# Table scatters in four pairs, each released by a cast on ScalarE, in a routed-expert transformer layer

## The chip, the cores and the metric

The kernel runs on one core of a Trainium2 chip. The metric is the device time of one execution in microseconds (us), as the median of several runs. The engines of the core are TensorE (PE, matmuls), VectorE (DVE), ScalarE (ACT), GpSimd (POOL) and SyncE (SP, which here issues most of the plain DMA transfers). Each works through its own queue in order and waits for the others by semaphores.

## The reference, cut to what matters

Eight sequences of 512 tokens with 256 features pass a cross attention (16 heads) and then a mixture of eight experts, of which each token takes its two best. Everything is float32.

```python
x = x + tanh(g_xattn[0]) * xattn(layernorm(x), ctx, ctx, mask, wq, bq, wk, bk, wv, bv, wo, bo)
x_flat = layernorm(x).reshape(-1, D)                 # 4096 tokens, D = 256
probs = softmax(x_flat @ router_w + router_b)        # E = 8 experts
top_w, top_idx = top_k(probs, 2)
comb = sum(top_w[..., None] * one_hot(top_idx, E), axis=1)
for e in range(E):
    h = gelu(x_flat @ expert_up[e].T)                # 1024 wide
    output = output + comb[:, e:e+1] * (h @ expert_down[e].T)
x = x + tanh(g_ffn[0]) * output
```

## The kernel before

**Routing by a table in HBM.** The kernel computes for each token only its two experts. When the router's choice for a batch (one sequence, four tiles of 128 tokens) is known, each of the batch's 1024 token-expert pairs gets a place in a table in HBM: the expert's region plus the number of pairs that the expert has so far. `place` (L343 to L374) works these places out. PE counts along the partitions (L348, L349), ACT copies the counts (L351), and POOL adds the running totals `filled` (L354, L355), picks the two places per token (L359 to L366, result `at`), writes the entries (token numbers L368, weight L371), and casts all eight columns of places to integers (L374, `place_i`). `enter(t)` (L376 to L382) then scatters tile t's entries, two indirect DMAs on POOL's queue (L378), one for each of the token's two choices. A batch has four such calls, so eight scatters.

**Expert jobs.** Experts are computed in jobs s of at most 256 table lines. Job s passes these steps:
- `list_rows(s)`, list(s) for short: SP reads the job's lines from the table (L690) into `listed`. It waits for every scatter that stands ahead of it in the program, and a scatter that stands behind it waits until it has read.
- `load(s)`: SP loads the expert's matrices up(s) and down(s), 1 MB each (L702, L703); there are three buffers.
- `fetch(s)`: POOL gathers the normalized token rows xg(s) by two indirect DMAs (L708); `turn(s)`: PE transposes them (L724), DVE copies them out (L726).
- `ups(s)`: PE multiplies with up (L736, h_ps, five PSUM banks), ACT applies GELU (L740, hT).
- `fetch_y(s)`: POOL gathers the rows of the output so far, y(s), by two indirect DMAs (L708). They must find the rows that job s-1 wrote.
- `downs(s)`: for each half of the job PE multiplies with down (L754, o_ps, two PSUM banks shared with other work), DVE scales and adds to y (L757), and POOL scatters the rows back (L760): out(s), two halves.

**The order of the work.** `attend_near` (L808) runs rounds b = -1 to 7. Round b does attention of batch b, prepares batch b+1 and b+2, projects and routes batch b-1, and enters batch b-2 into the table. A round has four groups g and in each three places n; a plan says which steps stand at (g, n) (L952 to L1003). The expert steps of jobs 0 to 3 stand at fixed groups of rounds 4 to 7 (`amid`, L1015 to L1030): the first lists at the end of round 4 (`begin`, L1006), list(5) and list(6) at the start of round 7's last group. Jobs from 4 on run after the last round, in what is called the tail here (L1080 to L1092); there the rest of batch 7's routing, and the placing and entering of batches 6 and 7, are taken from a queue, one step after each expert step. Entering before the change:

```python
for place, enter, counts in behind_route:
    plan[0, 2].append(place)
    if counts:
        plan[0, 2] += enter + counts
    else:
        for where, step in zip(((0, 2), (1, 0), (1, 1), (1, 2)), enter):
            plan[where].append(step)
```

`counts` are the planner's steps (L614 to L671), on DVE, that decide which lines a stage of jobs takes; they come with batches 2, 5 and 7. The order in which an engine's instructions are issued is made by a scheduler from this program: it may move an instruction ahead or back where data allows it, unless the instruction is wrapped in `keep_in_program_order`, which holds it at its place among its engine's instructions. The four `enter` calls were not held so, and on POOL all eight scatters of batches 0 to 5 ended up side by side behind the cast L374.

Only this branch runs with the inputs at hand (the mask's window is narrow); `attend_anywhere` (L1095) uses the same `finish` but isn't executed.

Of the kernel before, what the change touches and what calls it, by code (L numbers as in the profile page):

```python
# [24 lines left out]
QT = S // P  # L25
# [38 lines left out]
def flamingo_layer(ctx: ExitStack, tc: tile.TileContext, a: dict, out: bass.AP):  # L64
    nc = tc.nc
# [80 lines left out]
    place_i = fixed([P, B * QT, 2], "place_i", I32)  # L146
# [94 lines left out]
    def shared(p2, small, bank):  # L241
# [39 lines left out]
        def finish(b):  # L281

            x2T = p2.tile([P, DC, S], F32, tag="xnT", name=f"x2T{b}", bufs=1)
            said = {}

            def t3(name, dtype=F32):
                return small.tile([P, QT, E], dtype, tag=name, name=f"{name}{b}", bufs=2)

            def t2(name):
                return small.tile([P, QT], F32, tag=name, name=f"{name}{b}", bufs=2)  # L290

            def keep_rows(xn):
                nc.sync.dma_start(out=token_rows(rows, b), in_=xn)

            def keep_x():
                nc.sync.dma_start(out=token_rows(out, b), in_=xs[b])

            def logits():

                ps = bank(f"route_ps{b}")[:, :P]  # L300
                for dc in range(DC):
                    for t in range(QT):
                        nc.tensor.matmul(
                            ps[32 * t : 32 * t + 32, :], lhsT=rw[:, dc, :], rhs=x2T[:, dc, t * P : (t + 1) * P],
                            start=(dc == 0), stop=(dc == DC - 1),
                        )
                said["lgT"] = small.tile([P, P], F32, tag="lgT", name=f"lgT{b}", bufs=1)
                nc.scalar.copy(said["lgT"], ps)

            def route():  # L310
                ps = bank(f"lg_ps{b}")[:, :P]
                nc.tensor.transpose(ps, said["lgT"], ident)
                lg = t3("lg")
                nc.vector.tensor_tensor(
                    lg, ps.rearrange("p (t e) -> p t e", t=QT)[:, :, :E], over_t(rb), ALU.add
                )
                mx = t2("mx")
                nc.vector.tensor_reduce(mx, lg, AX.X, ALU.max)
                nc.vector.tensor_tensor(lg, lg, over_e(mx), ALU.subtract)
                pr = t3("pr")  # L320
                nc.scalar.activation(pr, lg, AF.Exp)
                sm = t2("sm")
                nc.vector.tensor_reduce(sm, pr, AX.X, ALU.add)
                rs = t2("rs")
                nc.vector.reciprocal(rs, sm)
                nc.vector.tensor_tensor(pr, pr, over_e(rs), ALU.mult)
                top = t3("top")
                idx = t3("idx", U32)
                for t in range(QT):
                    nc.vector.max(top[:, t, :], pr[:, t, :])  # L330
                    nc.vector.max_index(idx[:, t, :], top[:, t, :], pr[:, t, :])
                ix = t3("ix")
                nc.vector.tensor_copy(ix, idx)
                picks = small.tile([P, QT, 2, E], F32, tag="picks", name=f"picks{b}", bufs=2)
                nc.vector.tensor_tensor(
                    picks, iota.unsqueeze(1).unsqueeze(1).to_broadcast([P, QT, 2, E]),
                    ix[:, :, :2].unsqueeze(3).to_broadcast([P, QT, 2, E]), ALU.is_equal,
                )
                both = t3("both")
                nc.vector.tensor_tensor(both, picks[:, :, 0, :], picks[:, :, 1, :], ALU.add)  # L340
                said["top"], said["picks"], said["both"] = top, picks, both

            def place():  # L343

                both = said["both"].rearrange("p t e -> p (t e)")
                ps = bank(f"place_ps{b}")
                n = QT * E
                nc.tensor.matmul(ps[:, :n], lhsT=before, rhs=both, start=True, stop=True)  # L348
                nc.tensor.matmul(ps[:, n : 2 * n], lhsT=ones, rhs=both, start=True, stop=True)  # L349
                counts = small.tile([P, 2, QT, E], F32, tag="counts", name=f"counts{b}", bufs=2)  # L350
                nc.scalar.copy(counts.rearrange("p i t e -> p (i t e)"), ps[:, : 2 * n])  # L351
                place = t3("place")
                for t in range(QT):
                    nc.gpsimd.tensor_tensor(place[:, t, :], counts[:, 0, t, :], filled, ALU.add)  # L354
                    nc.gpsimd.tensor_tensor(filled, counts[:, 1, t, :], filled, ALU.add)  # L355
                mine = slice(b * QT, (b + 1) * QT)
                at = small.tile([P, QT, 2], F32, tag="at", name=f"at{b}", bufs=2)
                picked = said["picks"]
                nc.gpsimd.tensor_tensor(  # L359
                    picked, picked, place.unsqueeze(2).to_broadcast([P, QT, 2, E]), ALU.mult  # L360
                )
                for k in (4, 2, 1):
                    nc.gpsimd.tensor_tensor(
                        at.unsqueeze(3) if k == 1 else picked[..., :k], picked[..., :k], picked[..., k : 2 * k],
                        ALU.add,
                    )  # L366
                entry = entries[:, b % 2]
                nc.gpsimd.tensor_copy(  # L368
                    entry[:, :, :, :2], tokens_i[:, mine].unsqueeze(2).unsqueeze(3).to_broadcast([P, QT, 2, 2])
                )  # L370
                nc.gpsimd.tensor_scalar(  # L371
                    entry.bitcast(F32)[:, :, :, 2], said["top"][:, :, :2], tg[:, 1:2], None, ALU.mult
                )
                nc.gpsimd.tensor_copy(place_i[:, mine, :], at)  # L374

            def enter(t):  # L376
                for i in range(2):
                    nc.gpsimd.indirect_dma_start(  # L378
                        out=table_parts[2 * t + i][:, :],
                        out_offset=bass.IndirectOffsetOnAxis(ap=place_i[:, t, i : i + 1], axis=0),  # L380
                        in_=entries[:, b % 2, t % QT, i, :], in_offset=None,
                    )  # L382

            places = [place] + [lambda t=t: enter(t) for t in range(b * QT, (b + 1) * QT)]
            return x2T, keep_x, keep_rows, logits, route, places

# [421 lines left out]
    def attend_near(att):  # L808
# [230 lines left out]
        for b in range(-1, B):  # L1039
            if b + 3 < B:  # L1040
                load_x(b + 3, p2)
            if b + 3 < B:
                load_win(b + 3)
            if b == -1:
                clear_table(p2.tile([P, S], I32, tag="raw", name="none", bufs=1))
            behind_route = list(later)
            later.clear()
            if b == 0:
                looks, settle = normalize((2, "a", lambda: xnT[2]))
            plan = between(*(n if 0 <= n < B and (b, n) != (-1, 2) else None for n in (b - 1, b + 2, b + 3)))  # L1050
            if b == 0:
                plan[0, 0] += looks
                plan[0, 1].insert(0, settle)
            for place, enter, counts in behind_route:
                plan[0, 2].append(place)
                if counts:
                    plan[0, 2] += enter + counts
                else:
                    for where, step in zip(((0, 2), (1, 0), (1, 1), (1, 2)), enter):
                        plan[where].append(step)  # L1060
            for g in range(4):
                c, i = g // 2, g % 2
                if b >= 0:
                    pT = weights_T(b, c, i)
                work = deque(amid.get((b, g), []))
                for n in range(3):
                    if n == 0 and behind is not None:
                        weigh(*behind)
                    if n == 1 and b + 1 < B:
                        find_tops(b + 1, c, i)  # L1070
                    if n == 2 and g >= 2 and b + 1 < B:
                        lower_tops(b + 1, 0, g - 2)
                    if n == 2 and g < 2 and b >= 0:
                        lower_tops(b, 1, g)
                    for _ in range(-(-len(work) // (3 - n))):
                        work.popleft()()
                    for step in plan[g, n]:
                        step()
                behind = (b, c, i, pT) if b >= 0 else None
# [340 lines left out]
```

## Time and profile before

| what | us |
|---|---|
| median of 3 runs (lowest, highest) | 834.48 (833.77, 834.83) |
| the profiled execution | 850.71 |
| its span, first to last instruction | 848.9 |
| PE busy | 767.4 |
| DVE busy | 326.6 |
| POOL busy | 313.8 |
| ACT busy | 253.6 |
| 64 table scatters L378 on POOL | 62.7 (0.98 each) |
| 8 casts L374 on POOL | 0.19 each |
| first and last table scatter | 134.3, 447.9 |

Times within the execution are counted from the start of the span. A line of a timeline gives start, duration, engine, line of the kernel, operation, what it writes and reads, the shape, how many were merged, and in brackets the idle time ahead of it on its engine and what ended it ("issue": nothing that the profile shows). A line of the table by stretches gives from:to, the length, the busy time of PE, PE's weight loads, DVE, ACT and POOL with counts, the granted PE clock (1.00 is full), the share of the DMA engines, and GB/s. The busy shares, the granted clock and the DMA traffic over the span in 40 slices of 21.2 us:

```profile
PE   3786989888889999999997899999999999999992
DVE  7486887877865747524230111101011101011100
ACT  2434555453635435253311112121211111111210
POOL 2021115151645252545464453534353433434332
PEclk9788998998989999999999899999999999999997
DMA  4700001120292314063647557575666775747511
```

Each digit is a tenth. Up to slice 12 (250 us) PE and DVE are both busy, then DVE and ACT thin out as expert jobs take over, and from slice 22 on PE works through the jobs with everything else beside it. The scatters lie in slices 6 to 21.

### The profile page before, as it was taken

Reading aid. Unit: us, or ns where it says so; the run is one execution under the profiler, and the core shown is the slowest. Engines: PE = TensorE matmul, PEld = TensorE weight load, DVE = VectorE, ACT = ScalarE, POOL = GpSimd, SP = SyncE. Lnnn points to the kernel's source line nnn. Section 1 sums busy time; section 2 is a strip of 40 time slices with the busy share of each in tenths; the row PEclk is TensorE's granted clock in tenths of the full one; section 3 lists DMA queues with packets and bytes.
Section 4 is the critical chain, followed back from the end, with each engine's and each line's share of the span. In section 5 each row is a group of like instructions: output and inputs, shape, how many; then the busy total and the mean of one; then the engine's idle time right before and its main releaser. Section 6 shows DMA issues by size and latency. Waiting matters only on the chain. (4 is left out here: it accounts for less than half of the span.)

```text
span 848.9 us, 11331 instructions
## 1 busy us (share of the span) xinstructions
PE 767.4 (90%) x4090; PEld 568.3 (67%) x4090; DVE 326.6 (38%) x958; ACT 253.6 (30%) x485; POOL 313.8 (37%) x422
## 2 busy tenths in 40 slices
PE   3786989888889999999997899999999999999992
PEld 1343544444446575668786788888898988788882
DVE  7486887877865747524230111101011101011100
ACT  2434555453635435253311112121211111111210
POOL 2021115151645252545464453534353433434332
PEclk9788998998989999999999899999999999999997
DMA  4700001120292314063647557575666775747511
GB/s 143 259 7 1 32 32 32 47 68 12 87 316 95 106 53 125 4 211 94 215 133 261 197 162 244 171 240 164 228 183 227 219 253 169 243 164 245 198 50 36
DMA packets 87910, 121.58 MB, mean 143 GB/s; under 512 B 16798, under 2 KB 71713, under 8 KB 87841
## 3 DMA queue, kind: packets, MB, share of 16 engines
q1 hardware_dynamic: 75184, 93.44, 33.1%
q0 software_dynamic: 11840, 26.76, 10.2%
q8 instruction: 36, 0.59, 0.3%
q10 hardware_dynamic: 816, 0.53, 0.2%
q14 instruction: 34, 0.27, 0.1%
HBM read 101.05 MB, written 20.17 MB: 143 GB/s over the span
## 5 line engine op out<-in xcount | busy, mean ns | idle before, releaser
L754 PE MATMUL o_ps<-down,hT 128*128 128x256 f32 x1088 | 245.2, 383 | 10.9 <-DVE y L757 9.6
L736 PE MATMUL h_ps<-xT,up 128*128 128x256 f32 (+1 forms) x1152 | 243.9, 368 | 3.4 <-DMA up<-in_upT 1.7
L754 PEld LDWEIGHTS o_ps<-down,hT 128*128 128x128 f32 x1088 | 205.4, 192 | 43.8 <-DVE y L757 11.0
L736 PEld LDWEIGHTS h_ps<-xT,up 128*128 128x128 f32 x1152 | 208.1, 190 | 33.9 <-issue 5.2
L740 ACT ACTIVATE hT<-h_ps 128x512 f32<-128x512 f32 (+1 forms) x144 | 82.2, 573 | 366.5 <-PE h_ps L736 322.2
L757 DVE SCALAR_TENSOR_TENSOR y<-o_ps,listed,y 128x256 f32<-128x256 f32 x68 | 32.5, 482 | 285.7 <-DMA y<-out,listed 125.8
L708 POOL DMA_INDIRECT y<-out,listed x68 | 66.2, 974 | 153.8 <-DMA out<-y,listed 125.6
L760 POOL DMA_INDIRECT out<-y,listed x68 | 68.8, 1012 | 112.3 <-DVE y L757 77.6
L873 DVE TENSOR_REDUCE tops<-t_ps 128x4 f32<-128x512 f32 x128 | 79.4, 680 | 23.5 <-PE t_ps L868 20.2
L903 ACT ACTIVATE n_pT<-w_ps 128x512 f32<-128x512 f32 x128 | 67.8, 597 | 55.5 <-PE w_ps L898 48.3
L708 POOL DMA_INDIRECT xg<-rows,listed x68 | 64.9, 955 | 41.3 <-issue 17.7
L378 POOL DMA_INDIRECT table<-entries,place_i x64 | 62.7, 980 | 26.0 <-issue 16.5
L726 DVE COPY xT<-x_ps 128x512 f32<-128x512 f32 (+1 forms) x36 | 23.6, 657 | 97.7 <-PE x_ps L724 95.9
L898 PE MATMUL w_ps<-ql,km 32*128 32x512 f32 x256 | 60.0, 714 | 0.6 <-DVE tops L873 0.6
L850 POOL TENSOR_TENSOR x<-x,bo 128x1024 f32<-128x1024 f32 x8 | 18.7, 2344 | 67.1 <-issue 36.5
L868 PE MATMUL t_ps<-k,q 32*128 32x256 f32 x512 | 40.8, 408 | 1.7 <-ACT q L574 0.8
L937 PE MATMUL proj_ps<-woT,oT 128*128 128x256 f32 x128 | 32.8, 393 | 9.8 <-DVE oT L930 9.8
L916 PE MATMUL n_av<-n_pT,nv 128*32 128x512 f32 x256 | 40.0, 701 | 1.7 <-DVE xT L726 1.7
L868 PEld LDWEIGHTS t_ps<-k,q 32*128 32x128 f32 x512 | 25.3, 189 | 23.8 <-issue 16.5
L922 DVE STREAM_TRANSPOSE raw<-n_av 128x512 f32<-128x512 f32 x32 | 22.8, 713 | 44.9 <-PE n_av L916 31.4
L937 PEld LDWEIGHTS proj_ps<-woT,oT 128*128 128x128 f32 x128 | 23.2, 192 | 20.8 <-DVE oT L930 11.4
L570 PE MATMUL q_ps<-n_xnT,wqT 128*128 128x512 f32 x64 | 33.0, 643 | 0.0
(187 smaller groups left out, 559.0 us busy)
## 6 DMA issues: line engine op xcount, KB each, us to landing
up<-in_upT SPq DMA_DIRECT2D x36, 1024.0 KB
down<-in_downT SPq DMA_DIRECT2D x36, 1024.0 KB
out<-x SPq DMA_DIRECT2D x8, 512.0 KB
rows<-xn_f SPq DMA_DIRECT2D x8, 512.0 KB
x<-in_x SPq DMA_DIRECT2D x7, 512.0 KB
table<-none SPq DMA_DIRECT2D x1, 2288.0 KB
xg<-rows,listed POOLq DMA_INDIRECT x68
y<-out,listed POOLq DMA_INDIRECT x68
```

Source lines behind the costliest of these rows:

```text
L378: nc.gpsimd.indirect_dma_start(out=table_parts[2 * t + i][:, :], out_offset=bass.IndirectOffsetOnAxis(ap=place_i[:, t, i : i + 1], axis=0) ...
L708: nc.gpsimd.indirect_dma_start(out=dst, out_offset=None, in_=src[: seen[JOBS[s][0]], :], in_offset=bass.IndirectOffsetOnAxis(ap=listed[:, ...
L736: nc.tensor.matmul(ps[:, i, :n], lhsT=up[:, dc, (f + i) * P : (f + i + 1) * P], rhs=xT[:, dc, :n], start=(dc == 0), stop=(dc == DC - 1),)
L740: nc.scalar.activation(made[s][:, f : f + 2, :n], ps[:, :, :n], AF.Gelu)
L754: nc.tensor.matmul(ps, lhsT=hT[:, f, h * P : (h + 1) * P], rhs=down[:, f, :], start=(f == 0), stop=(f == FC - 1))
L760: nc.gpsimd.indirect_dma_start(out=out_parts[h][:, :], out_offset=bass.IndirectOffsetOnAxis(ap=listed[:, n, h, 0:1], axis=0), in_=y[:, h, ...
L868: ins = nc.tensor.matmul(ps[j][:, u], lhsT=q[rows_j, c, t * P : (t + 1) * P], rhs=k[rows_j, c], start=True, stop=True)
L873: nc.vector.tensor_reduce(top[:, 2 * tp : 2 * tp + 2, :].rearrange("p t (i x) -> p t i x", i=2)[:, :, :, 32 * j], ps[j], AX.X, ALU.max,)
L898: ins = nc.tensor.matmul(ps[j], lhsT=km[rows_j, c, i, :], rhs=lowered[b, c][rows_j, i, :], start=True, stop=True)
L903: nc.scalar.activation(pT[:, j, :], ps[j], AF.Exp)
L916: ins = nc.tensor.matmul(av[32 * j : 32 * j + 32, :], lhsT=made_of(b)[3][:, 8 * c + 2 * j + r, :], rhs=pT[:, j, :], start=True, stop=True,)
L937: nc.tensor.matmul(ps[:, t - ts[0], :], lhsT=outs[b, c][:, t * P : (t + 1) * P], rhs=w["woT"][:, c, :], start=(c == 0), stop=(c == DC - 1),)
```

## The change

The cast of a batch's places leaves `place` and POOL. In its stead `enter(t)` begins with a cast of its own tile's two columns, on ACT, held at its place in ACT's program order; the tile's two scatters need its result. There are now four casts of 128x2 per batch in place of one of 128x8. Further, the four `enter` calls of a batch are planned at (2,0), (2,1), (2,2) and (3,0) of the round in every round; before they stood at (0,2), (1,0), (1,1) and (1,2), or all at (0,2) in rounds with planner steps. The planner's steps stay at (0,2). In the tail the queue of steps is as before, and each `enter` in it begins with its cast.

```diff
@@ -371,9 +371,11 @@
                 nc.gpsimd.tensor_scalar(
                     entry.bitcast(F32)[:, :, :, 2], said["top"][:, :, :2], tg[:, 1:2], None, ALU.mult
                 )
-                nc.gpsimd.tensor_copy(place_i[:, mine, :], at)
+                said["at"] = at
 
             def enter(t):
+
+                tc.keep_in_program_order(nc.scalar.copy(place_i[:, t, :], said["at"][:, t % QT, :]))
                 for i in range(2):
                     nc.gpsimd.indirect_dma_start(
                         out=table_parts[2 * t + i][:, :],
@@ -1053,11 +1055,9 @@
                 plan[0, 1].insert(0, settle)
             for place, enter, counts in behind_route:
                 plan[0, 2].append(place)
-                if counts:
-                    plan[0, 2] += enter + counts
-                else:
-                    for where, step in zip(((0, 2), (1, 0), (1, 1), (1, 2)), enter):
-                        plan[where].append(step)
+                plan[0, 2] += counts
+                for where, step in zip(((2, 0), (2, 1), (2, 2), (3, 0)), enter):
+                    plan[where].append(step)
             for g in range(4):
                 c, i = g // 2, g % 2
                 if b >= 0:
```

At (7, 3), n = 0, the expert steps are taken ahead of the plan's steps, so list(5) and list(6) now stand in the program between batch 5's third and fourth `enter`; before, all four came earlier.

## The prediction

> **What bounds the kernel now.** I read the rows per slice first, then TensorE's (PE's) waits, then the timelines of PE, GpSimd (POOL), SyncE (SP) and ScalarE (ACT), since the change moves work on the last three. PE is busy 767.4 of 848.9 us. Up to 250 us it shares the load with VectorE (39.22 of 50 us busy from 50 to 100), in the middle attention and expert jobs mix, and from 470 us PE runs almost without a gap. So the end is set by when PE reaches that unbroken stretch. The last thing that holds it up is this (waits of PE between 430 and 520 us: total, times, longest):
>
> ```profile
> PE o_ps L754 <- DVE y L757: 6.3, 1, 6.3
> PE h_ps L736 <- DMA up<-in_upT: 1.7, 1, 1.7
> ```
>
> Both come from POOL and SP. POOL issues every table scatter, token gather xg(s), fetch y(s) and row scatter out(s) of expert job s in one order; SP's list(s) reads the table and so waits for all scatters written ahead of it in the program, and SP's loads stand behind the list. POOL, batch 5 and what follows it:
>
> ```profile
> 348.69 0.19 POOL L374 CAST place_i<-at 128x8 int32<-128x8 f32 x1
> 349.16 1.07 POOL L378 DMA_INDIRECT table<-entries,place_i  x1 [0.28 <-POOL place_i L374]
> ...
> 358.13 0.96 POOL L378 DMA_INDIRECT table<-entries,place_i  x1 [0.30 <-issue]
> ...
> 361.28 1.00 POOL L760 DMA_INDIRECT out<-y,listed  x1 [0.56 <-DVE hv_f L230]
> 363.17 0.99 POOL L708 DMA_INDIRECT xg<-rows,listed  x1 [0.90 <-issue]
> ...
> 372.32 0.94 POOL L708 DMA_INDIRECT y<-out,listed  x1 [4.28 <-DMA out<-y,listed]
> ...
> 378.54 1.02 POOL L760 DMA_INDIRECT out<-y,listed  x1 [2.77 <-DMA y<-out,listed]
> 380.02 1.01 POOL L760 DMA_INDIRECT out<-y,listed  x1 [0.47 <-DVE y L757]
> 383.27 0.98 POOL L708 DMA_INDIRECT y<-out,listed  x1 [2.24 <-issue]
> ...
> 387.28 0.20 POOL L354 TENSOR_TENSOR place<-counts,filled 128x8 f32<-128x8 f32 x1 [1.40 <-ACT counts L351]
> ```
>
> Eight scatters take 10 us of POOL right behind the places; out(2) comes after them; place(6) had only 1.4 us of slack. SP and ACT at that time:
>
> ```profile
> 360.54 1.20 SPq L690 DMA_DIRECT2D listed<-table  x2
> 364.97 1.08 ACT L255 ACTIVATE xn_f<-x,shift_f,rstd_end_f 128x256 f32<-128x256 f32 x2
> 391.00 0.60 ACT L740 ACTIVATE hT<-h_ps 128x512 f32<-128x512 f32 x1 [2.97 <-PE h_ps L736]
> 392.73 0.60 ACT L740 ACTIVATE hT<-h_ps 128x512 f32<-128x512 f32 x1 [1.13 <-PE h_ps L736]
> ```
>
> **Part 1, casts.** Eight POOL casts of 0.19 go (1.5 us of POOL, nobody waits on the saving). ACT gains 32 casts of 128x2. Nearest row: ACT's copy of counts, 128x64, 0.21 us; neighbours on ACT overlap by about 0.1 (302 to 304 us: a 0.60 GELU, the copy 0.50 after its start). So 0.1 to 0.2 each. PE's and VectorE's orders are untouched in the branch that runs. In rounds 2, 3, 4 one cast stands ahead of q and two ahead of the last exponentials (149.37 us in round 2), and PE's n_av, which took 1.93 us there (150.93) against 1.06 at 158.73, is paced by these. Round 6 has three casts ahead of the exponentials at 323.83; in round 5 they fall into a 0.86 us wait of ACT; in round 7 one reaches x2T, for which PE waited 1.17. On the path: 13 casts, 1.3 to 2.6 us if all is passed on, 0 if VectorE's own lag hides it; I take **+1.5**, an estimate.
>
> **Part 2, the first list (round 4).** list(0) was issued at 226.74, when the eighth scatter (224.41) had landed. Now the last pair waits for a cast behind x2T, which ends at 236.9: cast to 237.2, two scatters to 239.8, landing 1.3 later (225.37 to 226.67), so list(0) at 241.1, 14.4 later, and with it loads and gathers. xg(0) goes out at 243.6 (list to gather 2.5, as at 226.74 to 229.26) and PE wants it at 250.36. The second half leaves at 244.9, beside 4 MB of loads; gathers and fetches under such load land after 5.9 to 6.7 us (463.71; 413.92), so at 251. up(0) is then issued at 242.8, wanted at 256.9. I take **+0.7**, an estimate between 0 (landing in 3 us, as 831.59 to 834.41 near the end) and 3.
>
> **Part 3, rounds 5 and 6** cost nothing: in round 5 out(1) and y(1) keep the times that VectorE and the landings give them (284.3, 290.5), since the last pair is out by 288. In round 6 out(1)'s second half waits for a store of x anyway (327.68), six scatters follow to 336.5, and y(2) goes from 333.5 to 336.5; VectorE wants it at 352.2, so 10 us of cover remain beside its landing.
>
> **Part 4, round 7 and the tail.** Here the order of the changed POOL queue is: place(5), out(2), y(3), six scatters, xg(5), two scatters, xg(6), out(3), y(4), place(6). The durations are those above: 1.26 per scatter, 2.6 from list to gather, 3.3 from out(3) to y(4), 4.0 from y(4) to place(6).
> - Gain: out(2) at 352.8 and 354.6, once y(2) is added, and y(3) at 358.5 instead of 372.3. PE hardly gets any of it: VectorE's wait for y(3), 5.80 us at 376.93, held PE nowhere (its o_ps at 372.05 waited for x2T).
> - Loss: the first cast stands behind xn_f, 366.05. Scatters run 366.5 to 373.8, list(5) at 375.1 (was 360.54), xg(5) 377.8, last pair to 382.9, xg(6) to 385.6, out(3) at 385.9 and 387.4 (was 378.54, 380.02), y(4) 390.7, place(6) 393.3, places ready at 396.6 instead of 390.6: **6.0 late**. up(5), issued at 377, is still early for 393.9.
> - New wait: ACT reaches batch 6's first cast at 391.6 and stands until 396.6, with hT of 392.73 and the GELUs from 396.00 queued behind it. PE needs that hT for o_ps at 401.36 and has five h_ps banks, so this alone costs 0; if place(6) slipped another 5 us it would be paid one for one.
> - On from there: scatters 397.3; list(7) 403.5 (was 397.67); up(6) 404.5, landed after 5.3 (as 451.11 to 456.37) at 409.8, wanted at 407.84; list(8) 414.5 (was 408.74); out(4)'s second half 419.8 (was 415.25); y(5) 426.4; place(7) 429.0 (was 424.43); list(9) 436.9; out(5)'s second half 440.7 (was 437.37), as one scatter and not two precedes it; y(6) 447.3; last scatters to 453.8; list(10) 455.2 (was 450.34); out(6)'s second half 460.2 (was 457.09); y(7) 466.8 (was 463.71), landed and added 6.5 later. PE's o_ps of 470.22 starts at 473.3: **+3.1**. PE's new gaps for up(6), up(8), up(9) (about 2, 1.4 and 3.2 us) lie inside this and are not added. Ends: -2.0 (were place(6) not late, the new order alone brings out(6) forward by some 2) and +6.0 (all the lateness passed on). Nearest row for the gaps kept is the same queue before, hence 3.1.
>
> **Sum** on the profiled run: 850.71 + 1.5 + 0.7 + 3.1 = 856.0. The median shown is 16.2 us below the profiled time; the difference of 5.3, carried over, gives 834.48 + 5.3, about **840**.
>
> **Two rules weighed.** (a) The Trainium skill, "SBUF — State Buffer" (the "DVE blocks DMA" trap): while VectorE holds the port pair in a fast mode, GpSimd can't write descriptors, and a 620 ns DMA became 3100. It would make it matter among which VectorE work a scatter falls, by up to 2.5 us each. The row says no: 64 scatters last 954 to 1194 ns, median 959, with VectorE busy at 80% or at 10%. By the row this is 0, and I take the row. (b) "TensorE: Matmul & The Clock Gate", Part 1: after an idle window of about 3.4 us the clock halves. The row agrees after the 6.27 us wait:
>
> ```profile
> 470.00:475.00 5.00, 4.78 (x11) 3.88 (x12) 1.15 (x3) 0.00 (x0) 2.02 (x2) 0.50 0.15 52
> ```
>
> (the last three numbers are granted clock, DMA share and GB/s: clock 0.50; that o_ps took 9.64 us against 6.91 for the next). One such restart is in the time already. By the rule each new gap over 3.4 would cost about 2.7 more, by the row's reading only the gap that ends last does; my gap for up(9) is 3.2. I take 0 and leave 2.7 to 5.4 to the range.
>
> **Rivals.** (1) *Faster.* Row scatters freed from the burst: if place(6) starts within 1.5 us of 387.28, the tail keeps its times, out(6) leaves some 2 us sooner and the 6.27 us wait with its cold restart (2.7) shrinks or goes. At most 9.0 back against 2.2 for parts 1 and 2: about 828. For it: 14 us gained on y(3). Against: xg(5) and out(3) stand behind pairs that ACT lets go only at 366. It decides at place(6). (2) *Cover holds*: the profiled run is 16 us longer than the median, and if that lies in DMA and POOL, the tail's POOL has slack otherwise, so that only casts and the first list are paid: about 836.5. (3) *Worse*: the late loads open two or three cold gaps, or ACT's wait for the places reaches hT in time to stop PE: 10 more than the forecast, 850. (4) The change not doing what it says: POOL's built order does show the pairs apart, each waiting for ACT; I give it nothing of its own.
>
> **Chances.** Forecast 840 (own range 837 to 845) 0.50; rival 1 0.13; rival 2 0.20; rival 3 0.17. A measurement of this kernel tells 0.2% (1.7 us) from no change, so same is 832.8 to 836.2; it gets 0.08, out of rival 2. Faster 0.13, slower 0.79. Range 832.5 to 849: it leaves out most of rival 1 and the upper part of rival 3.
>
> **What will show it.** list(0) near 241 and list(5) near 375; place(6) near 393 plus the casts' shift; ACT waiting for POOL's at by some 5 us near 392; y(3) near 358; PE's last long wait ending about 5 us later than 470.2. It is wrong if place(6) keeps to 388, or if list(5) does not wait for the six scatters, or if PE already stops at 250 for xg(0) by over 3 us.

## The result, and the profile after

The changed kernel took 839.98 us (median; 837.67 to 845.67) beside 833.04 us for the kernel before (827.74 to 834.83) in the same comparison: ratio 1.0097, 95% interval 1.0069 to 1.0125. It is 7 us slower by the medians, 8 by the ratio. A second comparison later gave 1.0080 (1.0047 to 1.0114).

I read PE's waits first, between 90 and 480 us of the changed kernel (what PE waited for: total, times, longest, in us):

```profile
PE x_ps L726 <- DMA xg<-rows,listed: 5.6, 2, 4.8
PE h_ps L738 <- DMA up<-in_upT: 5.3, 3, 3.1
PE o_ps L756 <- DVE y L759: 5.2, 2, 4.3
```

The first line is new: before, PE waited for no gather of tokens there. The second has grown from 1.7 us in one wait to 5.3 in three. The third has shrunk from 6.3. The timeline of the changed kernel around the first (start, duration, engine, line; in brackets the idle time before it and what ended that):

```profile
198.20 1.97 PE L939 MATMUL proj_ps<-woT,oT 128*128 128x256 f32 x6 [3.07 <-DVE oT L932]
...
218.71 1.04 POOL L380 DMA_INDIRECT table<-entries,place_i  x1 [12.82 <-ACT place_i L378]
...
228.22 0.96 POOL L380 DMA_INDIRECT table<-entries,place_i  x1 [0.30 <-issue]
...
230.45 1.29 SPq L692 DMA_DIRECT2D listed<-table  x2
233.66 1.01 POOL L710 DMA_INDIRECT xg<-rows,listed  x1 [3.01 <-DMA listed<-table]
...
240.24 0.48 PE L726 MATMUL x_ps<-ident,xg 128*128 128x128 f32 x1 [4.76 <-DMA xg<-rows,listed]
...
246.96 2.00 PE L939 MATMUL proj_ps<-woT,oT 128*128 128x256 f32 x8
```

POOL has the places of batch 2 and stands idle for 12.82 us until ACT comes to the first cast; the last scatter leaves at 228.22, SP's list(0) right after its landing, the gather at 233.66, and PE stands until its first half is there. In the tail of the same execution:

```profile
356.48 1.00 POOL L380 DMA_INDIRECT table<-entries,place_i  x1 [6.07 <-ACT place_i L378]
...
365.29 1.27 SPq L692 DMA_DIRECT2D listed<-table  x2
...
375.46 1.02 POOL L762 DMA_INDIRECT out<-y,listed  x1 [0.31 <-DVE picks L335]
...
383.00 0.21 POOL L354 TENSOR_TENSOR place<-counts,filled 128x8 f32<-128x8 f32 x1
...
451.26 8.83 PE L738 MATMUL h_ps<-xT,up 128*128 128x256 f32 x32 [3.13 <-DMA up<-in_upT]
464.86 8.86 PE L756 MATMUL o_ps<-down,hT 128*128 128x256 f32 x32 [4.33 <-DVE y L759]
```

These starts can't be set beside those of the profile before as they stand: up to the n_av of the last round the execution profiled there, itself 16 us over its median, needed 10 us more than this one. The next section shows how the two are lined up.

### The profile page after: what moved, and what is told of

Its sections match the earlier page's. It is cut to its first block, busy times and chain, and to the rows that moved or that the text cites. A ratio compares the mean times of both kernels' runs of the same rounds, so it can differ in the third digit from the quotient of the medians.

```text
span 844.0 us, 11352 instructions
## 1 busy us (share of the span) xinstructions
PE 760.6 (90%) x4090; PEld 565.4 (67%) x4090; DVE 326.2 (39%) x958; ACT 253.9 (30%) x517; POOL 312.0 (37%) x414
## 5 line engine op out<-in xcount | busy, mean ns | idle before, releaser
L710 POOL DMA_INDIRECT xg<-rows,listed x68 | 65.1, 958 | 35.5 <-issue 17.8
L900 PE MATMUL w_ps<-ql,km 32*128 32x512 f32 x256 | 53.5, 717 | 0.0
L939 PE MATMUL proj_ps<-woT,oT 128*128 128x256 f32 x128 | 33.6, 398 | 10.7 <-DVE oT L932 10.7
L918 PE MATMUL n_av<-n_pT,nv 128*32 128x512 f32 x256 | 38.0, 669 | 1.7 <-DVE xT L728 1.7
```

The costliest lines, as they stand in the source:

```text
L710: nc.gpsimd.indirect_dma_start(out=dst, out_offset=None, in_=src[: seen[JOBS[s][0]], :], in_offset=bass.IndirectOffsetOnAxis(ap=listed[:, ...
L900: ins = nc.tensor.matmul(ps[j], lhsT=km[rows_j, c, i, :], rhs=lowered[b, c][rows_j, i, :], start=True, stop=True)
L918: ins = nc.tensor.matmul(av[32 * j : 32 * j + 32, :], lhsT=made_of(b)[3][:, 8 * c + 2 * j + r, :], rhs=pT[:, j, :], start=True, stop=True,)
L939: nc.tensor.matmul(ps[:, t - ts[0], :], lhsT=outs[b, c][:, t * P : (t + 1) * P], rhs=w["woT"][:, c, :], start=(c == 0), stop=(c == DC - 1),)
```

## The experiments

**A second profile of the kernel before.** No edit.

> The kernel before, profiled a second time. In the two profiles so far the pass from the proj_ps wait of round 2 to that of round 4 took 72 us after the change and 82 us before it, and the later pieces carry that offset of about 10 us. Theory A (run-to-run: the profiled execution of before was itself 17 us over its median, with PE at half clock in 147-155 and 187-195): this second execution takes 72 to 76 us for the same pass, a span near 834, and x_ps in round 4 does not wait for a gather by more than 1 us. Rival B (the later, parted scatters really free 10 us in rounds 2 and 3, and the change loses 17 elsewhere): the pass takes 81 to 83 us again. Time equal to before within 0.2% by both.

Measured: 829.43 us, ratio 0.9988 (0.9961 to 1.0015). In its trace the pass from proj_ps of round 2 (125.19) to that of round 4 (199.74) takes 74.6 us, where the first profile had 81.7. Theory A holds in so far as the profile that I predicted from was of an execution in which PE took longer over these rounds than in this one and in all later ones near 832 us (71.8 to 72.0 with batches 0 and 1 held). Its 850.71 us lies far outside 827 to 839, the range of the kernel before in every comparison but one, and inside that of the other one, from another chip (844.79 to 856.33, told below). On which chip the first profile was taken is not on record, so whether it differs by the execution or by the chip stays open.

To compare traces I therefore use three marks on PE: **M1**, the proj_ps of round 2 that waits 3.07 us for oT; **M2**, the n_av of the last round that waits 1.66 us for xT; **M3**, the o_ps that ends the last long wait of the tail. Two stretches then hold all that the change touches:

| kernel | M1 to M2 | M2 to M3 | ratio of times to before |
|---|---|---|---|
| before, first profile | 233.6 | 110.9 | |
| before, second profile | 218.3 | 110.7 | |
| changed | 223.1 | 115.4 | 1.0097 |
| changed, again | 223.0 | 114.5 | 1.0080 |
| batches 2 and 5 as before | 215.9 | 109.6 | 0.9969 |
| batch 2 as before | 216.0 | 115.1 | 1.0036 |
| batch 5 as before | 222.9 | 109.5 | 1.0036 |
| batches 2 and 5 early, on ACT | 215.4 | 110.8 | 0.9951 |
| tail cast on POOL | 222.7 | 115.9 | 1.0124 |
| all batches early, on ACT | 225.5 | 109.9 | 1.0101 |

(all from runs on chips where the kernel before takes 831 to 833 us, but the first line; after M3 the traces take 373 to 380 us more, which does not follow the kernels: the two profiles of before have 378.7 and 373.4.)

**Batches 2 and 5 as before.** Their lists and gathers follow at once, those of the other batches don't.

```diff
+                if b in (2, 5):
+                    nc.gpsimd.tensor_copy(place_i[:, mine, :], at)
...
+                if b not in (2, 5):
+                    tc.keep_in_program_order(nc.scalar.copy(place_i[:, t, :], said["at"][:, t % QT, :]))
...
+                if b - 2 in (2, 5):
+                    plan[0, 2] += enter + counts
+                else:
+                    plan[0, 2] += counts
...
```

> The changed kernel, but batches 2 and 5, the last of each pass over a chunk whose lists and gathers follow at once, get their places cast on POOL and all eight scatters behind the place step, as before. Theory A (what the change costs is the late list and gathers behind batches 2 and 5: PE's x_ps wait of 5.6 us in round 4 and the 4.5 us by which the tail came out later): nearly all of the 8 us goes, 831 to 836 us, ratio 0.998 to 1.003, and the x_ps wait for xg falls under 1 us. Rival B (each ACT cast costs, by its own time and by ACT's waits for POOL): 24 of 32 casts stay, so some three quarters of the loss stays, 838 to 840, ratio 1.006 to 1.008. Rival C (only the tail of batches 6 and 7 matters): nothing moves, 840 to 842, ratio 1.009 to 1.011.

Measured: 829.51 us, ratio 0.9969 (0.9946 to 0.9992). All of the loss goes, and a little more, with 24 of the 32 casts still on ACT. PE's waits:

```profile
PE o_ps L759 <- DVE y L762: 5.8, 1, 5.8
PE h_ps L741 <- DMA up<-in_upT: 1.7, 1, 1.7
```

There is no line for x_ps, and that for up is back at one wait of 1.7 us. Theory A stands; B and C, which wanted 1.006 and more, fall.

**Only batch 2, only batch 5 as before.** The same edit with one batch.

> The changed kernel with only batch 2 as before. Theory A: the x_ps wait in round 4 (5.6 us in the trace) goes, the tail's 4.5 us stay: 835 to 838 us, ratio 1.003 to 1.006. My prediction's own sum had only 0.7 us for that wait; by it the ratio would be 1.008 to 1.010. Rival B (casts as such): 28 of 32 stay, ratio 1.008 to 1.009.

> The changed kernel with only batch 5 as before. Theory A: list(5), out(3), y(4) and the place step of batch 6 are no longer late against the work around them, so the tail regains 3 to 4.5 us and the x_ps wait of round 4 stays: 835.5 to 837.5 us, ratio 1.003 to 1.006; y(3) goes back behind out(2) near the end of the list. Rival B (casts as such): 28 of 32 stay, ratio 1.008 to 1.009. If early y(3) is worth something to the tail, this kernel gives it up, and the ratio stays above 1.007.

Measured: 1.0036 (1.0016 to 1.0055) and 1.0036 (1.0013 to 1.0058), as Theory A has it. From these and the run before it, holding batch 2's scatters costs 1.0036 - 0.9969 = 0.67%, 5.6 us, and holding batch 5's as much (each ratio is known to some 0.2%, so these 5.6 us to 2 or 3). The table shows each in its own stretch: batch 2's 7 us in M1 to M2, batch 5's 5.5 in M2 to M3.

**Early pairs on ACT.** All 32 casts stay on ACT; only the places of batches 2 and 5 in the plan move.

```diff
-                for where, step in zip(((2, 0), (2, 1), (2, 2), (3, 0)), enter):
+                for where, step in zip((((1, 0), (1, 0), (1, 1), (1, 1)) if b - 2 in (2, 5) else ((2, 0), (2, 1), (2, 2), (3, 0))), enter):
```

> The changed kernel, all 32 casts still on ACT and all scatters still in pairs, but the pairs of batches 2 and 5 are put two at (1, 0) and two at (1, 1) instead of (2, 0) to (3, 0), so that ACT reaches them before the exponentials of the third piece. Theory A (only how late the lists of batches 2 and 5 come decides): x_ps of round 4 waits under 1 us for xg, the tail's waits for up fall back to about 1.7, and the time is that of the kernel with batches 2 and 5 as before, 828 to 833 us, ratio 0.995 to 1.001. Rival (an ACT cast in those two rounds costs by itself, since ACT waits there for POOL and PE for ACT): the time stays above 835, ratio 1.004 to 1.010, although the lists are early.

This run fell on another chip: 865.4 us beside 849.41 for the kernel before, ratio 1.0195 (1.0157 to 1.0232). It went against Theory A, but its trace has waits that, of the earlier ones, only the first profile of before has, and that one far less. ACT's, from 130 to 420 us:

```profile
ACT lgT L308 <- remote: 26.2, 4, 10.7
...
ACT n_pT L905 <- remote: 13.9, 2, 11.6
```

"remote" stands where the profile finds nothing on the core that released the wait. While ACT stood for its 10.7 us before 334.45 us, PE waited 8.64 us for lgT and VectorE stood as well, and POOL issued its scatters at their usual pace. So I ran the same kernel again beside the changed one:

> The changed kernel once more, so that the two next runs have it on their own chip: the last four runs came from a chip on which the kernel before takes 849 instead of 832 us and on which the trace shows engines idle until something that it names remote (63 us of it on ACT, DVE together in the kernel with the early pairs, none in the six traces of the other chip). On a chip like the first: 838 to 842 us, ratio 1.007 to 1.011, x_ps waits 5 to 6 us in round 4. On a chip like the second: 857 to 865, ratio 1.010 to 1.018, with remote waits of some 5 us at ACT's lgT in the rounds whose scatters are in pairs.

> The pairs of batches 2 and 5 early, still cast on ACT, as before on the second chip. Theory A (how late the lists of batches 2 and 5 come decides) on a chip like the first: no x_ps wait over 1 us, up waits at 1.7, 828 to 833 us, ratio 0.995 to 1.001. Rival (the ACT casts of these two rounds cost by themselves): ratio 1.004 to 1.010. On a chip like the second both are covered by the remote waits, and the run decides only against the changed kernel beside it: at least 0.8% below it by Theory A, within 0.4% of it by the rival.

Measured: the changed kernel 1.0080 (1.0047 to 1.0114), the early pairs 828.68 us and 0.9951 (0.9928 to 0.9973), without remote waits. In its timeline:

```profile
203.13 1.04 POOL L380 DMA_INDIRECT table<-entries,place_i  x1 [0.85 <-ACT place_i L378]
...
213.21 0.96 POOL L380 DMA_INDIRECT table<-entries,place_i  x1 [0.30 <-issue]
...
215.51 1.28 SPq L692 DMA_DIRECT2D listed<-table  x2
...
231.74 0.60 PE L726 MATMUL x_ps<-ident,xg 128*128 128x128 f32 x4
```

POOL waits 0.85 us for ACT instead of 12.82, list(0) leaves 20.9 us after round 4's proj_ps (194.59), and x_ps has no bracket: the tokens lay there. One wait for up, of 3.2 us where 1.7 was expected, is left in the tail. With the casts all on ACT and only their places moved, the loss is gone: what costs in these two rounds is how late the casts come and not that ACT makes them. The rival falls on this chip; why the same kernel loses on the other one stays open.

**The tail's casts on POOL.** `if b in (6, 7)` casts on POOL, else as changed.

> The changed kernel, but batches 6 and 7, whose places are made in the tail, are cast on POOL as before; batches 0 to 5 as changed. My prediction put no cost on the tail's casts themselves: then 839 to 841 us, ratio 1.009 to 1.011, and PE's waits for up (5.3 us) and y stay as they are. Rival (the lateness of the tail comes from the parted scatters of batches 6 and 7): 835 to 837, ratio 1.003 to 1.006, and the waits for up fall to 1.7.

On the other chip: 862.79 us, 1.0139 (1.0099 to 1.0179), with 26.4 us of remote waits of lgT. Again beside the changed kernel:

> Batches 6 and 7 cast on POOL as before, 0 to 5 as changed. My prediction put no cost on the tail's casts: within 0.3% of the changed kernel beside it, on either chip. Rival (the parted scatters of batches 6 and 7 make the tail late): 0.4 to 0.6% below it, and PE's waits for up fall to 1.7.

Measured 1.0124 (1.0084 to 1.0164) against 1.0080 for the changed kernel there. The intervals overlap. The rival wanted it 0.4 to 0.6% below; by the medians it is 0.4% above, just past the 0.3% that I had allowed. The longest wait for up did fall, to 1.8 us, but PE's waits for y rose to 8.6 us instead, and M2 to M3 stayed at 115.9. The parted scatters of batches 6 and 7 are not the cause.

**Only batches 0 and 1, only batches 6 and 7 changed.** Both on that other chip.

> The kernel before with batches 0 and 1 alone as changed (scatters in rounds 2 and 3). The kernel with batches 2 and 5 as before came out 0.31% under before, and in its trace the pass from the proj_ps wait of round 2 to the n_av wait of the last round is 2.4 us shorter. If that comes from the scatters of rounds 2 and 3, this kernel has the same pass 2 to 3 us shorter than before's 218.3 and the time is 829.5 to 831, ratio 0.996 to 0.999. If it is the clock of the one execution, the pass is within 1 us of before's and the ratio 0.999 to 1.001.

> The kernel before with batches 6 and 7 alone as changed (scatters in the tail). With batches 2 and 5 as before the tail, from the n_av wait to the end of the last long o_ps wait, took 109.6 and 109.5 us against before's 110.7 and 110.9. If the parted scatters of batches 6 and 7 give this 1.1 us: 109.5 here, and 830.5 to 832 us, ratio 0.998 to 1.000. If batches 3 and 4 give it: 110.7 here, ratio 0.999 to 1.001.

Measured 0.9938 (0.9917 to 0.9960) and 1.0023 (0.9995 to 1.0050). The first says that entering batches 0 and 1 in the new way saves time, there 0.6%. The expectation's length of the pass can't be used, since the pass is long on that chip: 230.3 us from M1 to M2 here, 235.9 with only 6 and 7 changed. The second shows no gain from batches 6 and 7, and its M2 to M3 is 111.0, so the 1.1 us shorter tails with batch 5 as before stay unexplained.

**All batches early.** `((1, 0), (1, 0), (1, 1), (1, 1))` for every batch.

> All batches' pairs early, two at (1, 0) and two at (1, 1), still cast on ACT. With only batches 2 and 5 early the kernel came out at 0.9951 of before, 4 us under it, which my prediction has no step for. If that gain comes from the late scatters of batches 0, 1, 3 and 4 in their rounds, it goes here: ratio 0.998 to 1.001, and the pass from the proj_ps wait of round 2 to the n_av wait of the last round is 218, as in before. If it comes from the casts' leaving POOL or from holding the scatters in two steps at all, it stays: ratio 0.994 to 0.997, pass near 215.5. Theory A's part, no x_ps wait for xg over 1 us, holds by both.

Measured 840.95 us, 1.0101 (1.0061 to 1.0141): slower, for a reason that neither side of the expectation had. The timeline in round 5:

```profile
250.03 0.29 ACT L378 CAST place_i<-at 128x2 int32<-128x2 f32 x2 [10.83 <-POOL at L363]
...
253.25 1.22 PE L553 MATMUL k_ps<-pick,kn 128*128 128x128 f32 x4 [7.23 <-ACT n_xnT L266]
```

In round 5 POOL is late with the places of batch 3, as gathers for the first jobs stand ahead of them. ACT, in order, waits 10.83 us at the cast, with GELUs and the copy n_xnT queued behind, and PE waits 7.23 us for that copy. The x_ps wait is gone here as well. Behind the wait PE runs at a granted clock of 0.50 (252 to 256 us), and from round 4's last proj_ps to M2 this kernel takes 112.5 us where the second profile of before takes 102.8. Without these 9.7 us the pass would be 215.8, near the 215.5 of the expectation's second case, so the gain does not hang on late scatters. Where it lies is told under Part 1 below.

## Why the prediction came out right, and where it didn't

The forecast of about 840 was met (839.98), but partly by terms that cancel.

**Part 4, round 7 and the tail: mechanism right, size 1.4 short in the trace, 2.5 by the times.** Each start counted from M2, in the first profile of before and in the changed one:

| step | before | changed | later by | predicted |
|---|---|---|---|---|
| list(5) | 1.2 | 15.8 | 14.6 | 14.6 |
| out(3), first half | 19.2 | 26.0 | 6.8 | 7.4 |
| place(6) | 27.95 | 33.55 | 5.6 | 6.0 |
| list(7) | 38.3 | 43.6 | 5.3 | 5.8 |
| list(10) | 91.0 | 95.5 | 4.5 | 4.9 |
| y(7) | 104.4 | 108.5 | 4.1 | 3.1 |
| o_ps, M3 | 110.9 | 115.4 | 4.5 | 3.1 |

The chain of queues is the one written down beforehand; only its last links gave back less than I took. PE's gaps for up came (0.80, 1.33 and 3.13 us against about 2, 1.4 and 3.2). y(3) came 14.3 us sooner and brought nothing, and ACT waited 4.6 us for the places of batch 6 (5 predicted) without PE losing anything. Rival 1 was decided where it said, at place(6), 5.6 us late and not within 1.5.

**Part 2, the first list, is the step that failed: the +0.7 us taken for it, "an estimate between 0 [...] and 3".** It measured 5.6 us of waiting in the trace, 7 us of the stretch, 5.6 of the time. That PE stops for xg(0) by over 3 us was one of the signs named beforehand for being wrong, and it came. The lateness of list(0) itself was right (32.25 us after round 4's proj_ps instead of 19.3, so 13.0 late; 14.4 predicted), and so was the landing of the gather (6.6 us, 233.66 to 240.24; 5.9 to 6.7 predicted). Wrong was when PE would want the tokens. I read 250.36 from the first profile, 42.9 us after the same proj_ps. The second profile of before:

```profile
199.74 1.56 PE L937 MATMUL proj_ps<-woT,oT 128*128 128x256 f32 x6 [3.07 <-DVE oT L930]
...
219.03 1.28 SPq L690 DMA_DIRECT2D listed<-table  x2
...
221.66 1.01 POOL L708 DMA_INDIRECT xg<-rows,listed  x1 [2.48 <-PE q_ps L570]
...
236.99 0.60 PE L724 MATMUL x_ps<-ident,xg 128*128 128x128 f32 x4
...
240.75 1.99 PE L937 MATMUL proj_ps<-woT,oT 128*128 128x256 f32 x8
```

Here PE is at x_ps 37.25 us after proj_ps, and the changed kernel's PE was ready after 37.3 (240.24 - 4.76 - 198.20). In all nine traces near 832 us PE is ready for x_ps 37.1 to 37.6 us after that proj_ps. The first profile's execution had given the gather 5.7 us of cover that a usual one doesn't have, enough for all of the 4.9 us by which the wait was missed. Rival 2 had noticed that the profile was 16 us too long, and drew the opposite from it, that cover elsewhere was larger than it looked.

**The cold clock, taken as 0.** After that wait PE ran at half clock, which the sum did not pay for and the range left room for. The changed kernel from 240 to 247 us (its last three numbers: granted clock, DMA share, GB/s):

```profile
240.00:247.00 7.00, 5.93 (x25) 2.41 (x25) 0.69 (x1) 1.97 (x5) 5.80 (x14) 0.51 1.05 368
```

From the ready x_ps to the next proj_ps takes 11.5 us in the changed kernel (246.96 - 235.48) and 3.8 in the second profile of before (240.75 - 236.99). The waits explain 5.6 of these 7.7, and the rest, 2.1, is the same work done at 0.51 of the clock. So the rule weighed there, from the Trainium skill, "TensorE: Matmul & The Clock Gate", Part 1, counted once more than my reading of the row allowed: by the rule this gap costs one more restart, 2.7 as the prediction sized it, by my reading of the row nothing, and 2.1 were measured.

**Part 1, casts at +1.5: not seen.** With 24 casts on ACT the kernel is at 0.9969, with all 32 and two batches early at 0.9951. What the casts and the parted scatters together bring apart from batches 2 and 5 is 0.3% in favour, 2.6 us. The single casts take 0.1 to 0.3 us as predicted, but PE's waits for ACT between 90 and 480 us are, line by line, within 0.2 us of those in the second profile of before. No run has the casts without the parting, so the casts' own cost isn't measured.

Where the gain lies can be read. From round 3's proj_ps to round 4's PE takes 34.8 or 34.9 us in all eight traces near 832 us in which batches 0 and 1 are held, all pairs early included, and 37.3 in the second profile of before. The other pieces from M1 to M2 agree within 0.4 us, but for the x_ps wait with its slow stretch and the stop in round 5 with all pairs early. The difference stands right behind round 3's proj_ps, which waits 3.07 us for oT in both; from there to the next proj_ps, in the second profile of before and in the changed kernel (third number from the end: granted clock):

```profile
162.46:170.31 7.85, 7.34 (x31) 3.51 (x31) 5.23 (x14) 1.64 (x4) 2.64 (x13) 0.59 0.00 1
163.43:169.03 5.60, 4.63 (x30) 2.55 (x31) 5.23 (x14) 1.06 (x3) 1.21 (x6) 1.00 0.00 0
```

So the gain is, in these traces, one stretch of half clock that doesn't come, for which the prediction has no term. What keeps it away stays open, and so does how often an execution of before has it: in the first profile the clock is 1.00 there.

**Part 3** held: from round 4's last proj_ps to M2 the changed kernel takes 102.5 us, the second profile of before 102.8.

Added up by the times: 5.6 + 5.6 - 2.6 = 8.6, against 6.9 measured between the medians, 8.1 by the first ratio and 6.7 by the second; I had 0.7 + 3.1 + 1.5 = 5.3. Two terms were too small, and a cost of 1.5 stood where 2.6 were gained, so that the errors nearly cancelled; the rest came from the kernel before, which ran at 833.04 in this comparison and not at 834.48. That the number was met to the microsecond is luck.

Three smaller readings of the prediction don't hold as written, without weight for the sum. From y(4) to place(6) it counts 2.6 us and not the 4.0 that it lists (the wait of 1.4 is taken off; the trace has 2.58). The o_ps next to the one of 9.64 us takes 7.07 and not 6.91, so that restart cost 2.6. And 413.92, named among the landings of gathers, is the start of a row scatter.

**A version faster than both** on these chips is the one with early pairs for batches 2 and 5: 0.9951 of before. On the other chip it was the slowest of the four tried.

## What to carry to other kernels

When a release is moved into another engine's order, its place must be later than its data (or the engine stops, as in round 5 with all pairs early) and come before its consumers' slack ends; the batches whose results are used at once need another place than those whose results aren't. Before slack is read from a profile, set the profiled time beside the median: where it is 2% over, the slack of one execution is not that of the usual one, and a second profile of the unchanged kernel is worth more than finer arithmetic on the first.

## What the runs showed of the hardware

- **Chips differ, and not alike for all kernels.** On one chip the kernel before took 849.41 us (844.79 to 856.33) instead of 832, and all four kernels traced there have remote waits, 17.8 to 47.6 us of them on ACT; none of the nine traces taken with times near 832 us for the kernel before has one. The kernel with early pairs went from 0.9951 to 1.0195 of before. The first profile of before has some too (7.6 us on VectorE's raw, 4 on ACT). What they are stays open. In rounds 2 and 3 they come at lgT, for 5.1 to 5.2 us each, in the three kernels that have pairs there, and not in the fourth, which has none.
- **The same short gap is followed by half clock in one place and by full clock in another.** Behind a wait of 3.07 us the same stretch of PE's work took 7.85 us at a granted clock of 0.59 in round 3 of the second profile of before and 5.60 us at 1.00 in the changed kernel; in round 4 it is the other way round (5.60 at 1.00 before, 7.85 at 0.57 changed). In the tail h_ps took 8.83 us after a gap of 3.13 in the changed kernel and, with all pairs early, 8.76 after 2.20, both at 0.81; it took 7.14 at 1.00 after 3.21 with early pairs. By the Trainium skill, "TensorE: Matmul & The Clock Gate", Part 1, it takes an idle window of about 3.4 us, and the window runs freely; here gaps of 2.2 to 3.1 us were followed by slow stretches, though not every one, so the measured gaps decide. No run moved a gap against the window.
